# The choice of tokens in a four-layer kernel: lists in single instructions, a merge of minima and maxima, and an output norm in parts

## The chip, the cores and the metric

The kernel runs on one core of one Trainium2 chip as a single program. The metric is the device time in microseconds. The core has five engines with a queue each: TensorE (PE, with its weight loads shown as PEld), VectorE (DVE), ScalarE (ACT), GpSimd (POOL) and SyncE (SP), which issues most of the DMAs. Each engine works through its own queue in order; between engines there are semaphores.

## The reference

The input is 8 sequences of 512 rows of 256 numbers in float32. Four layers follow each other, and each adds a mixer and then a feed-forward part to the rows, both between layer norms. The change lies in the second layer. Its two parts are these, cut to what matters:

```python
# second mixer: 8 heads of 128, one common k and v, causal softmax
q = (x @ Wq + bq) + pe          # per head
k = kv[..., :128] + pe;  v = kv[..., 128:]
probs = softmax(causal(q @ k.T / sqrt(128)))
out = concat_heads(probs @ v) @ Wo
x = x + layernorm(out)

# second feed-forward part: 48 experts choose their tokens
xf = layernorm(x).reshape(4096, 256)
vals, idx = top_k((xf @ Wr.T).T, 128)       # 128 tokens for each of 48 experts
w = softmax(vals, axis=-1)
y = expert_mlp(xf[idx]) * w[..., None]      # gelu, 4 blocks of 256x256 and 256x64
out = zeros_like(xf).at[idx].add(y)
x = x + layernorm(out)
```

So every expert needs its 128 largest logits over all 4096 tokens, and no expert can start before the last sequence has left the mixer.

## The kernel before

The rows `X` stay in SBUF through the whole kernel, as 8 sequences of 128 partitions by 4 tiles by 256. The program is written in loops that are unrolled when it is built. A framework then orders each engine's queue: it lets an instruction go when what it needs is ready in its own account of the time, and prefers what comes earlier in the program. So the place of a step in the text is a rank and not a fixed slot.

**The mixer, `l1_attn`.** The outer loop runs over the sequences `b`, the next one over the heads `h`, the inner one over four query tiles `qt`. `scores` makes one matmul into PSUM (L927), a masked minimum on DVE (L932), the exponential with its sum on ACT (L936), a reciprocal on DVE (L937) and the scaling on POOL (L938). Two steps later `behind` transposes the tile on PE (L944) and copies it on ACT or DVE (L947, L949); after the fourth query tile `weigh` multiplies with V (L954, L957). After the eighth head `finish` projects with `wo` on PE (`project_out`, L193), and `add_norm` makes statistics (L105), an inverse root by three rounds of short DVE instructions (L90 to L96), `onb` (L170), four activations on ACT (L177) and one addition into `X` on POOL (L182). Between the heads, `front(b+1)` makes the next sequence's queries.

**The choice, class `Choice`.** Beside the attention of the following sequences, `logits` normalizes a finished sequence again, stores it to DRAM for the gathers, and makes its 48 router logits. The sequences go in five groups: (0,1), (2,3), (4,5), (6), (7). In a group, partitions 0 to 47 hold the experts' logits for the first sequence or half, and partitions 64 to 111 those of the second. `lists` takes the 128 largest of every row in 16 rounds of `max`, `max_index` and `match_replace` (L1076 to L1079). It is a generator: one step is one round of three instructions. `RATE[b]` is the number of steps that are placed in one head of sequence `b`, spread over its query tiles. A list ends with DMAs on SP that bring the upper half down (L1082, L1086) and copies into a table `TAB` of values and indices. From group 1 on, `merge` takes the 128 largest of the sorted lists so far in 16 more rounds of `max` and `match_replace` over 384 or 512 elements (L1110, L1112).

Group 4, the last sequence, has no attention to lie beside. In `l1_ffn`, after its logits and its list come its merge and then `slots`: exponentials and their sum; the softmax weights of all ten lists in `TAB` (POOL, L1132); the table's DMA to DRAM (L1133); the count of every list's entries above the 128th value; from the counts the place of each list's share; nine gathers of windows of the table (POOL, L1174), each followed by a predicated copy (L1180); two transposes, which give the weights `wT` and the token indices `iT`. Then the loop over the 48 experts starts with the gather of `xg` (L1229). Weights of three experts are loaded ahead on SP (L1225 to L1227).

In the mixer `add_norm` reads the projection from PSUM for the statistics and for the activations; it has two more arguments which another mixer uses:

```python
        t = pool.tile([P, NT, D], F32, tag=tag, name=f"yn{b}")
        for n, ps in enumerate(halves):                    # leave=True
            nc.scalar.copy(t[:, 2 * n:2 * n + 2, :], ps)
        if halves:
            ys = [t[:, n, :] for n in range(NT)]
        ...                                                # four activations
        m = NT // parts
        for n in range(0, NT, m):
            x = self.X[b][:, n:n + m, :]
            nc.gpsimd.tensor_tensor(x, x, t[:, n:n + m, :], ALU.add)
```

Of the kernel before, what the change touches and what calls it, by code (L numbers as in the profile page):

```python
# [9 lines left out]
F32 = mybir.dt.float32  # L10
# [858 lines left out]
def l1_attn(K):  # L869
# [10 lines left out]
    with ExitStack() as es:  # L880
# [14 lines left out]
        RATE = (0, 0, 1, 2, 3, 3, 5, 6)  # L895
# [63 lines left out]
        def finish(b):  # L959
            K.project_out(b, [(OT[b][:, h, :], wo[:, h, :]) for h in range(H)], pmm, "mm", s1)  # L960
# [41 lines left out]
class Choice:  # L1002
# [4 lines left out]

    E, NL, K = 48, 10, 128
    GROUPS = ((0, 1), (2, 3), (4, 5), (6,), (7,))

    def __init__(self, K):
# [10 lines left out]
        self.tab_d = dr.tile([E * NL * k, 2], F32, name="tab_d")  # L1022
# [15 lines left out]
        self.VV = cst.tile([E, NL, k], F32, name="VV")  # L1038
        self.TAB = cst.tile([E, NL * k, 2], F32, name="TAB")
        self.lg = {}  # L1040
        self.R = None
# [23 lines left out]
    def lists(self, g):  # L1065

        nc, E, k = self.kern.nc, self.E, self.K
        n = L if len(self.GROUPS[g]) == 2 else L // 2
        a = self.lg[g][:, 0:n]
        c = self.s1.tile([P, L], F32, tag="lg1", name=f"lga{g}")[:, 0:n]  # L1070
        val = self.sb.tile([P, k], F32, tag="val", name=f"val{g}")
        idx = self.sb.tile([P, k], U32, tag="idx", name=f"idx{g}")
        for r in range(k // 8):
            src, dst = (a, c) if r % 2 == 0 else (c, a)
            v8, i8 = val[:, 8 * r:8 * r + 8], idx[:, 8 * r:8 * r + 8]
            nc.vector.max(v8, src)  # L1076
            nc.vector.max_index(i8, v8, src)
            if r < k // 8 - 1:
                nc.vector.match_replace(dst, v8, src, -3.0e38)  # L1079
            yield  # L1080
        idf = self.sb.tile([P, k], F32, tag="idf", name=f"idf{g}")
        nc.sync.dma_start(out=self.VV[:, 2 * g + 1, :], in_=val[64:64 + E, :])  # L1082
        nc.vector.tensor_copy(idf, idx)
        nc.vector.tensor_scalar(idf, idf, self.first[:, g:g + 1], None, ALU.add)
        odd = self.sb.tile([E, k], F32, tag="odd", name=f"odd{g}")
        nc.sync.dma_start(out=odd, in_=idf[64:64 + E, :])  # L1086
        nc.vector.tensor_copy(self.VV[:, 2 * g, :], val[0:E, :])
        for j, t in enumerate((idf[0:E, :], odd)):
            lo = (2 * g + j) * k
            nc.gpsimd.tensor_copy(self.TAB[:, lo:lo + k, 1], t)  # L1090
        yield
        if g >= 1:
            yield from self.merge(g)

    def merge(self, g):

        nc, E, k = self.kern.nc, self.E, self.K
        if g == 1:
            lists = self.VV[:, 0:4, :]
        else:  # L1100
            nc.vector.tensor_copy(self.M[:, 1:3, :], self.VV[:, 2 * g:2 * g + 2, :])
            lists = self.M
        src = lists.rearrange("p l s -> p (l s)")
        n = src.shape[-1]
        two = [self.s1.tile([E, 4 * k], F32, tag=f"mg{j}", name=f"mg{g}_{j}")[:, 0:n]
               for j in range(2)]
        R = self.sb.tile([E, 3, k], F32, tag="R", name=f"R{g}")
        for r in range(k // 8):
            v8 = R[:, 0, 8 * r:8 * r + 8]
            nc.vector.max(v8, src)  # L1110
            if r < k // 8 - 1:
                nc.vector.match_replace(two[r % 2], v8, src, -3.0e38)  # L1112
                src = two[r % 2]
            yield
        self.M = R

    def slots(self, cst, sb, psum, ptag):

        K, nc = self.kern, self.kern.nc
        E, NL, k = self.E, self.NL, self.K  # L1120
        R = self.M[:, 0, :]

        nm = cst.tile([E, 1], F32, name="nm")
        nc.vector.tensor_scalar(nm, R[:, 0:1], -1.0, None, ALU.mult)
        sm = cst.tile([E, 1], F32, name="sm")
        ex = cst.tile([E, k], F32, name="ex")
        nc.scalar.activation(ex, R, AF.Exp, bias=nm, accum_out=sm)
        vv = self.VV.rearrange("p l s -> p (l s)")
        ev = cst.tile([E, NL * k], F32, name="ev")
        nc.scalar.activation(ev, vv, AF.Exp, bias=nm)  # L1130
        nc.vector.reciprocal(sm, sm)
        nc.gpsimd.tensor_scalar(self.TAB[:, :, 0], ev, sm, None, ALU.mult)  # L1132
        nc.sync.dma_start(  # L1133
            out=self.tab_d.rearrange("(e n) t -> e (n t)", e=E),
            in_=self.TAB.rearrange("p n t -> p (n t)"))

        thr = R[:, k - 1:k]
        cnt = []
        for op in (ALU.is_gt, ALU.is_ge):
            t = sb.tile([E, NL, k], F32, tag="cmp", name=f"cmp{len(cnt)}")  # L1140
            nc.vector.tensor_scalar(t.rearrange("p l s -> p (l s)"), vv, thr, None, op)
            c = cst.tile([E, NL], F32, name=f"cnt{len(cnt)}")
            nc.vector.tensor_reduce(c, t, AX.X, ALU.add)
            cnt.append(c)
        gt, eq = cnt
        nc.vector.tensor_tensor(eq, eq, gt, ALU.subtract)
# [13 lines left out]
        out = cst.tile([E, NL], F32, name="out")  # L1160
        nc.vector.tensor_tensor(out, end[:, 0:NL], end[:, 1:], ALU.subtract)
        nc.vector.tensor_scalar(out, out, float(k), None, ALU.add)

        at = cst.tile([E, NL], F32, name="at")
        nc.vector.tensor_tensor(at, self.start, end[:, 0:NL], ALU.subtract)
        ati = cst.tile([E, NL], U32, name="ati")
        nc.vector.tensor_scalar(at, at, 2.0, None, ALU.mult)
        nc.vector.tensor_copy(ati, at)
        got = cst.tile([E, k, 2], F32, name="got")
        nc.vector.tensor_copy(got, self.TAB[:, 0:k, :])  # L1170
        flat = self.tab_d.rearrange("n t -> (n t)")[:, None]
        for b in range(1, NL):
            t = cst.tile([E, 2 * k], F32, name=f"win{b}")
            nc.gpsimd.indirect_dma_start(  # L1174
                out=t, out_offset=None, in_=flat,
                in_offset=bass.IndirectOffsetOnAxis(ap=ati[:, b:b + 1], axis=0))
            m = cst.tile([E, k, 2], U8, name=f"from{b}")
            nc.vector.tensor_scalar(
                m, self.slot[:, :, None].to_broadcast([E, k, 2]), end[:, b:b + 1], None, ALU.is_ge)
            nc.vector.copy_predicated(got, m, t.rearrange("p (s t) -> p s t", t=2))  # L1180
        ps = psum.tile([P, 2, E], F32, tag=ptag, name="pgot")
        for j in range(2):
            nc.tensor.transpose(ps[:, j, :], got[:, :, j], K.ident[0:E, 0:E])
        wT = cst.tile([P, E], F32, name="wT")
        nc.vector.tensor_copy(wT, ps[:, 0, :])
        iT = cst.tile([P, E], U32, name="iT")
        nc.vector.tensor_copy(iT, ps[:, 1, :])
        return wT, iT

    def counters(self):  # L1190

        nc, cst, E, k = self.kern.nc, self.cst, self.E, self.K
        self.slot = cst.tile([E, k], F32, name="slot")
        self.start = cst.tile([E, self.NL], F32, name="start")
        for t, n, step, m in ((self.slot, k, 1, 0), (self.start, self.NL, k, self.NL * k)):
            i = self.s1.tile([E, k], I32, tag="io", name=f"io{m}")[:, 0:n]
            nc.gpsimd.iota(i, [[step, n]], base=0, channel_multiplier=m)
            nc.gpsimd.tensor_copy(t, i)

# [982 lines left out]
```

## Time and profile before

| What | Value |
|---|---|
| Median of 3 runs | 5109.19 us (5106.86 to 5115.65) |
| Profiled execution, its own time | 5105.01 us |
| Its span | 5103.3 us |
| Granted TensorE clock, mean | 0.933 |
| Busy: PE, DVE, ACT, POOL | 86%, 60%, 38%, 36% |
| First L932 of the mixer | 888.3 us from the span's start |
| Last L932 of the mixer ends | 1583.5 us |
| Last instruction of the last list ends | 1649.0 us |
| First gather of `xg` starts | 1694.6 us |
| Last gather of `xg` starts | 1983.3 us |

A line of the timeline has the start, the duration (of several alike, their stretch), the engine, the line of the kernel, the operation, what it writes and reads, the shapes and the count; in brackets the idle time before it and what ended it. A line of a table of windows has the stretch, its length, and each engine's busy time in it. Durations in groups are means of one instruction in nanoseconds. DVE's `max` appears as MAX8, `max_index` as a load and FIND_INDEX8, `match_replace` as a load and MATCH_REPLACE8; the masked minimum appears as CUSTOM_DVE_ANT_0.

### The profile page before, as it was taken

Reading aid. Unit: us, or ns where it says so; the run is one execution under the profiler, and the core shown is the slowest. Engines: PE = TensorE matmul, PEld = TensorE weight load, DVE = VectorE, ACT = ScalarE, POOL = GpSimd, SP = SyncE. Lnnn points to the kernel's source line nnn. Section 1 sums busy time; section 2 is a strip of 40 time slices with the busy share of each in tenths; the row PEclk is TensorE's granted clock in tenths of the full one; section 3 lists DMA queues with packets and bytes.
Section 4 is the critical chain, followed back from the end, with each engine's and each line's share of the span. In section 5 each row is a group of like instructions: output and inputs, shape, how many; then the busy total and the mean of one; then the engine's idle time right before and its main releaser. Section 6 shows DMA issues by size and latency. Waiting matters only on the chain.

```text
span 5103.3 us, 56570 instructions
## 1 busy us (share of the span) xinstructions
PE 4394.7 (86%) x18804; PEld 2694.8 (53%) x18804; DVE 3045.6 (60%) x8229; ACT 1958.5 (38%) x3835; POOL 1854.5 (36%) x1209
## 2 busy tenths in 40 slices
PE   8745788999895698899999999888888888799998
PEld 3334675555553697455555555433333333368884
DVE  6999746465778212666666543277777787751115
ACT  5411333434333233444444434365455555421112
POOL 0001212444433343211111110078778888803321
PEclk9877898999998899899999999999999999999999
DMA  4287421000001696000000000011111111126763
GB/s 114 79 198 177 130 64 56 5 5 9 5 14 40 171 249 173 5 5 5 5 5 5 1 21 1 1 54 45 42 44 44 50 46 42 56 71 226 235 206 103
DMA packets 401528, 357.89 MB, mean 70 GB/s; under 512 B 209394, under 2 KB 334020, under 8 KB 400676
## 3 DMA queue, kind: packets, MB, share of 16 engines
q1 hardware_dynamic: 373236, 305.83, 21.6%
q0 software_dynamic: 16320, 31.65, 2.2%
q10 hardware_dynamic: 11680, 16.80, 1.0%
q8 instruction: 149, 2.44, 0.2%
q14 instruction: 143, 1.17, 0.1%
HBM read 287.87 MB, written 66.09 MB: 69 GB/s over the span
## 4 chain that ended last, share of the span: by engine, by line
PE 37%; DVE 18%; issue 4%; POOL 4%; ACT 3%; DMA 1%; DVEq 0%; POOLq 0%; ACTq 0%; SPq 0%
DVE h L1730 7%; PE T L1432 5%; PE gb L1809 4%; DVE junk L1402 3%; PE h L1243 3%; PE g L1558 3%; PE y L1701 3%; PE yb L1823 2%; PE py L193 2%; DVE dB L1676 2%; PE pc L1623 2%; PE y L1254 2%; POOL h L1733 2%; PE o L1422 2%; PE pi L1609 1%
## 5 line engine op out<-in xcount | busy, mean ns | idle before, releaser
L1733 POOL TENSOR_TENSOR h<-h,C 128x1024 f32<-128x1024 f32 x256 | 595.8, 2354 | 175.6 <-DVE h L1730 141.9
L1701 PE MATMUL y<-h,C 128*128 128x512 f32 x1024 | 531.4, 660 | 107.1 <-POOL h L1733 107.1
L1730 DVE TENSOR_TENSOR_SCAN h<-dA,dB 128x512 f32<-128x512 f32 x512 | 589.0, 1203 | 29.4 <-ACT dA L1727 11.7
L1727 ACT ACTIVATE dA<-dl,A 128x512 f32<-128x512 f32 x512 | 352.5, 691 | 410.8 <-DVE h L1730 404.7
L1701 PEld LDWEIGHTS y<-h,C 128*128 128x128 f32 x1024 | 201.2, 208 | 414.5 <-issue 222.3
L938 POOL TENSOR_SCALAR p<-p,rs 128x128 f32<-128x128 f32 (+3 forms) x256 | 276.0, 1087 | 385.5 <-DVE rs L937 225.9
L1435 ACT ACTIVATE PT<-T 128x256 f32<-128x256 f32 (+3 forms) x512 | 212.1, 438 | 416.1 <-PE T L1432 396.0
L182 POOL TENSOR_TENSOR X<-X,yn 128x1024 f32<-128x1024 f32 (+1 forms) x80 | 154.1, 1932 | 590.3 <-ACT yn L177 529.3
L1397 PE MATMUL S<-KT,qz 128*128 128x512 f32 (+3 forms) x1024 | 326.0, 455 | 38.4 <-ACT qz L1385 16.9
L1432 PE MATMUL T<-qz,KT 128*128 128x512 f32 (+3 forms) x1024 | 318.1, 447 | 6.3 <-DVE mx L1402 4.2
L1437 POOL TENSOR_SCALAR_AFFINE_SELECT PT<-PT 128x512 f32<-128x512 f32 x128 | 81.8, 640 | 604.2 <-ACT PT L1435 599.8
L1681 POOL TENSOR_TENSOR dB<-du,B 128x2048 f32<-128x2048 f32 x64 | 289.6, 4525 | 0.1
L1402 DVE CUSTOM_DVE_ANT_0 junk<-S,mask 128x256 f32<-128x256 f32 (+3 forms) x512 | 249.8, 488 | 46.7 <-PE S L1397 2.6
L1397 PEld LDWEIGHTS S<-KT,qz 128*128 128x128 f32 x1024 | 178.5, 191 | 158.8 <-DVE mx L1402 36.7
L1809 PE MATMUL gb<-xbT,w_b 128*128 128x256 f32 (+1 forms) x1472 | 255.3, 332 | 1.0 <-ACT ts L2013 0.6
L1676 DVE TENSOR_TENSOR dB<-du,pb 128x2048 f32<-128x2048 f32 x64 | 145.4, 2273 | 167.2 <-PE pb L1673 117.5
L1815 DVE TENSOR_TENSOR hTb<-sb,gb 128x512 f32<-128x512 f32 x71 | 48.8, 687 | 325.4 <-PE gb L1809 325.4
L1809 PEld LDWEIGHTS gb<-xbT,w_b 128*128 128x128 f32 x1472 | 230.2, 191 | 23.1 <-ACT ts L2013 0.8
L1432 PEld LDWEIGHTS T<-qz,KT 128*128 128x128 f32 x1024 | 168.2, 191 | 121.5 <-issue 70.4
L936 ACT ACTIVATE p<-p,nm 128x128 f32<-128x128 f32 (+3 forms) x256 | 143.8, 563 | 198.5 <-DVE nm L932 193.3
L1248 ACT ACTIVATE hT<-h,w_l_ffn 128x128 f32<-128x128 f32 x384 | 109.8, 368 | 220.4 <-PE h L1243 220.4
L1243 PE MATMUL h<-xgT,w 128*128 128x128 f32 x1536 | 185.0, 279 | 0.0
(505 smaller groups left out, 9125.8 us busy)
## 6 DMA issues: line engine op xcount, KB each, us to landing
w_b<-l3f_w SPq DMA_DIRECT2D x138, 512.0 KB
w<-l1f_w SPq DMA_DIRECT2D x48, 1024.0 KB
C<-xdd SPq DMA_DIRECT2D x128, 256.0 KB
B<-xdd SPq DMA_DIRECT2D x64, 256.0 KB
w<-l1f_w SPq DMA_DIRECT2D x48, 256.0 KB
toep<-l0fd SPq DMA_DIRECT2D x32, 320.0 KB
X<-x SPq DMA_DIRECT2D x16, 512.0 KB
toep<-l0fd SPq DMA_DIRECT2D x32, 256.0 KB
```

The lines of the kernel that those rows point to most:

```text
L938: nc.gpsimd.tensor_scalar(p[:, 0:n], p[:, 0:n], rs, None, ALU.mult)
L1243: nc.tensor.matmul(ph[:, j, :], lhsT=w1[:, s, c, m * P:(m + 1) * P], rhs=xgT[:, c, :], start=(c == 0), stop=(c == 1))
L1397: nc.tensor.matmul(ps[:, 0:n], lhsT=QZ[:, j, qt * P:n], rhs=KT[:, g, 0:n], start=True, stop=True)
L1402: nc.vector.tensor_tensor_reduce(out=junk[:, 0:n], in0=tiles[j][:, 0:n], in1=mask[:, L - n:L], scale=1.0, scalar=-3.0e38, op0=ALU.add, op1 ...
L1432: nc.tensor.matmul(ps[:, 0:n], lhsT=KT[:, g, kt * P:(kt + 1) * P], rhs=QZ[:, j, kt * P:L], start=True, stop=True)
L1676: nc.vector.tensor_tensor(dB, du, pb[:, None, :].to_broadcast([P, 4, L]), ALU.mult)
L1681: nc.gpsimd.tensor_tensor(dB, du, B[:, None, :].to_broadcast([P, 4, L]), ALU.mult)
L1701: nc.tensor.matmul(py[2 * j + c], lhsT=K.ident, rhs=h[:, c, :], start=False, stop=(n == NS - 1))
L1727: nc.scalar.activation(dA, dl[:, c, :], AF.Exp, scale=A[:, c, n:n + 1])
L1730: nc.vector.tensor_tensor_scan(hs[-1][:, c % 2, :], dA, dB[:, c, :], 0.0, ALU.mult, ALU.add)
L1733: nc.gpsimd.tensor_tensor(h, h, C[:, None, :].to_broadcast([P, 2, L]), ALU.mult)
L1809: nc.tensor.matmul(ps[:, q, :], lhsT=ww[:, k, (c + q) * P:(c + q + 1) * P], rhs=xT[:, k, :], start=(k == 0), stop=(k == 1))
```

## The change

In the mixer, the projection's halves are copied from PSUM to SBUF on ACT before the activations read them, and the addition into `X` is made in four parts. `lists` yields after each instruction, and `RATE` counts instructions. The values are written into `VV` at once, the table `TAB` is kept on 128 partitions and holds raw values and indices, and each group's part goes to DRAM as soon as its list ends. Two sorted lists are merged by one maximum of the one with the reverse of the other, which leaves the 128 largest, and seven stages of a minimum and a maximum, which sort them again; the last list needs only the first of these. In `slots` the threshold is the minimum of the merged values, both halves are counted on 128 partitions, there are five gathers of 128 rows, the weights are computed from the gathered values, and each slot's share is picked by a product with a mask `own` and a matmul with `sel`, which adds the two halves and transposes. The diff, cut:

```diff
-        RATE = (0, 0, 1, 2, 3, 3, 5, 6)
+        RATE = (0, 0, 3, 5, 5, 5, 10, 9)
...
-            K.project_out(b, [(OT[b][:, h, :], wo[:, h, :]) for h in range(H)], pmm, "mm", s1)
+            K.project_out(
+                b, [(OT[b][:, h, :], wo[:, h, :]) for h in range(H)], pmm, "mm", s1, leave=True,
+                parts=4)
...
             nc.vector.max(v8, src)
+            yield
             nc.vector.max_index(i8, v8, src)
+            yield
             if r < k // 8 - 1:
                 nc.vector.match_replace(dst, v8, src, -3.0e38)
-            yield
+                yield
         idf = self.sb.tile([P, k], F32, tag="idf", name=f"idf{g}")
-        nc.sync.dma_start(out=self.VV[:, 2 * g + 1, :], in_=val[64:64 + E, :])
         nc.vector.tensor_copy(idf, idx)
-        nc.vector.tensor_scalar(idf, idf, self.first[:, g:g + 1], None, ALU.add)
+        nc.vector.tensor_scalar(
+            self.TAB[:, g, :, 1], idf, self.first[:, g:g + 1], None, ALU.add)
+        nc.scalar.copy(self.TAB[:, g, :, 0], val)
+        nc.sync.dma_start(
+            out=self.tab_d.rearrange("(p g s) t -> p g (s t)", p=P, g=len(self.GROUPS))[:, g],
+            in_=self.TAB[:, g].rearrange("p s t -> p (s t)"))
...
+        nc.vector.tensor_copy(odd, self.VV[64:64 + E, g, :])
         yield
-        if g >= 1:
-            yield from self.merge(g)
+        for j, x in enumerate((self.VV[0:E, g, :], odd)):
+            last = g == len(self.GROUPS) - 1 and j == 1
+            yield from self.merge(x, f"{g}_{j}", last)
...
+        if self.M is None:
+            self.M = x[:, ::-1]
+            return
+        t = self.sb.tile([E, k], F32, tag="mg", name=f"mg{uid}")
+        nc.vector.tensor_tensor(t, self.M, x, ALU.max)
+        s = k // 2
+        while s and not last:
+            u = self.sb.tile([E, k], F32, tag="mg", name=f"mg{uid}_{s}")
+            a, b = (v.rearrange("p (m h s) -> p m h s", h=2, s=s) for v in (t, u))
+            for h, op in enumerate((ALU.min, ALU.max)):
+                nc.vector.tensor_tensor(b[:, :, h, :], a[:, :, 0, :], a[:, :, 1, :], op)
+            t = u
+            s //= 2
+            if s in (16, 4, 1):
+                yield
+        self.M = t
+        yield
...
+        nc.vector.tensor_reduce(st[0:E, 0:1], R, AX.X, ALU.min)
+        nc.vector.tensor_copy(st[up, 0:1], st[0:E, 0:1])
...
+        for j, op in enumerate((ALU.is_gt, ALU.is_ge)):
+            t = cst.tile([P, G, k], F32, name=f"cmp{j}")
+            nc.vector.tensor_scalar(
+                t.rearrange("p l s -> p (l s)"), self.VV.rearrange("p l s -> p (l s)"),
+                st[:, 0:1], None, op)
+            nc.vector.tensor_reduce(cnt[:, j, :], t, AX.X, ALU.add)
...
-        for b in range(1, NL):
-            t = cst.tile([E, 2 * k], F32, name=f"win{b}")
+        for g in range(G):
+            t = cst.tile([P, k, 2], F32, name=f"win{g}")
             nc.gpsimd.indirect_dma_start(
...
+        pgot = [psum.tile([P, E], F32, tag=ptag, name=f"pgot{j}") for j in range(2)]
+        for j in (1, 0):
+            for g, t in enumerate(win):
+                v = sb.tile([P, k], F32, tag=f"v{j}", name=f"v{j}_{g}")
+                if j:
+                    nc.vector.tensor_tensor(v, t[:, :, 1], own[0][:, g, :], ALU.mult)
+                else:
+                    nc.scalar.activation(v, t[:, :, 0], AF.Exp, bias=st[:, 1:2])
+                    nc.vector.scalar_tensor_tensor(
+                        v, v, st[:, 2:3], own[0][:, g, :], ALU.mult, ALU.mult)
+                nc.tensor.matmul(
+                    pgot[j], lhsT=v, rhs=self.sel, start=(g == 0), stop=(g == G - 1))
```

## The prediction, made before the changed kernel ran

> **What bounds the kernel now.** The page's slices put the second mixer and its choice in slices 7 to 13 of 40. I cut that stretch with the table of windows. The edges are the moments at which DVE starts the masked minimum (L932) of head 0 of sequences 1 to 7. The columns are length, then busy time (and instructions) of PE, PEld, DVE, ACT and POOL, then the clock and DMA.
>
> ```profile
> core 0: us, PE busy (x) PEld busy (x) DVE busy (x) ACT busy (x) POOL busy (x), PEclk, DMA share, GB/s
> 957.60:1047.60 90.00, 84.49 (x354) 53.03 (x353) 42.41 (x194) 36.57 (x99) 38.28 (x34) 1.00 0.02 7
> 1047.60:1138.40 90.80, 85.07 (x355) 52.89 (x354) 64.93 (x255) 36.97 (x99) 38.14 (x34) 1.00 0.02 7
> 1138.40:1228.20 89.80, 84.47 (x354) 53.02 (x353) 49.65 (x213) 36.55 (x99) 38.88 (x36) 1.00 0.02 7
> 1228.20:1326.60 98.40, 87.28 (x354) 53.67 (x353) 71.91 (x277) 36.96 (x99) 38.84 (x36) 0.98 0.02 7
> 1326.60:1417.80 91.20, 84.46 (x354) 53.28 (x353) 61.42 (x236) 36.79 (x99) 38.34 (x34) 1.00 0.02 6
> 1417.80:1515.10 97.30, 87.14 (x354) 53.54 (x353) 72.69 (x282) 37.00 (x99) 38.83 (x36) 0.98 0.02 7
> ```
>
> PE sets the pace: a sequence without lists (1 and 3) takes 90 us. Sequences 4 and 6 take 8.4 and 7.3 us more, sequence 5 takes 1.2, sequence 2 only 0.8. In sequence 2 the list had 26.0 us of DVE (same table, tile `val` alone) at one round a head; in 4 it had 32.9 at three rounds a head. So list work in DVE's gaps is nearly free, and costs when it stands ahead of the attention's own instructions.
>
> After the last scores comes a tail. The windows from there to the first expert's gather:
>
> ```profile
> 1603.00:1612.40 9.40, 0.00 (x0) 0.00 (x0) 9.29 (x42) 0.04 (x1) 0.00 (x0) 0.61 0.00 0
> ...
> 1627.40:1650.60 23.20, 1.22 (x2) 0.50 (x2) 21.37 (x83) 0.00 (x0) 0.29 (x1) 0.53 0.33 90
> 1650.60:1669.60 19.00, 0.00 (x0) 0.00 (x0) 18.00 (x47) 1.36 (x1) 0.29 (x1) 0.50 0.01 1
> 1669.60:1680.10 10.50, 0.00 (x0) 0.00 (x0) 8.57 (x27) 1.78 (x3) 4.07 (x1) 0.50 0.23 47
> 1680.10:1694.60 14.50, 0.44 (x2) 0.31 (x2) 4.28 (x11) 0.00 (x0) 8.19 (x10) 0.50 0.14 31
> ```
>
> PE is idle: nothing else can run until the choice of tokens is known, so a microsecond off this chain is one off the span. In order: the last output norm; the last list; the last merge; counts and the table's way to memory; nine gathers. The timeline shows the first of these being held:
>
> ```profile
> 1610.28 0.55 DVE L1110 MAX8 R<-mg 48x8 f32<-48x384 f32 x1
> ...
> 1610.76 0.14 DVE L94 TENSOR_TENSOR onw<-onh,ony 128x4 f32<-128x4 f32 x1
> ...
> 1610.95 0.53 DVE L1112 MATCH_REPLACE8 mg<-R,mg 48x384 f32<-48x384 f32 x1
> ...
> 1612.17 0.16 DVE L170 SCALAR_TENSOR_TENSOR onb<-onmv,ony 128x4 f32<-128x4 f32 x1
> 1612.36 1.93 ACT L177 ACTIVATE yn<-py,onb,ony 128x256 f32<-128x256 f32 x4 [20.29 <-DVE onb L170]
> 1614.38 2.34 POOL L182 TENSOR_TENSOR X<-X,yn 128x1024 f32<-128x1024 f32 x1 [21.62 <-ACT yn L177]
> ```
>
> Group 3's merge alternates with the norm's short chain, and the one addition of 2.34 us waits for all four activations. Inside a sequence that addition has another effect (timeline of sequence 1):
>
> ```profile
> 986.71 2.36 POOL L182 TENSOR_TENSOR X<-X,yn 128x1024 f32<-128x1024 f32 x1
> ...
> 989.10 1.40 DVE L105 BATCH_NORM_STATS2 lnst<-X 128x6 f32<-128x256 f32 x4 [1.91 <-POOL X L182]
> ...
> 990.70 0.13 DVE L937 RECIPROCAL rs<-rs 128x1 f32<-128x1 f32 x1
> ...
> 991.00 2.78 POOL L938 TENSOR_SCALAR p<-p,rs 128x384 f32<-128x384 f32 x2 [1.94 <-DVE rs L937]
> ...
> 992.30 0.55 PE L944 MATMUL t<-C,p 128*128 128x128 f32 x3 [1.73 <-DVE lny L91]
> ```
>
> DVE waits for the addition, the reciprocals stand behind it, then POOL, then PE for 1.73 us.
>
> **Part 1, the choice after the last list.** Before: the last list instruction ends at 1649.0 and the first gather `xg` starts at 1694.58, 45.6 us. After, step by step:
> - Index cast, offset, copy of the upper half: 0.75 (from 1649.04 to 1649.58, and a 0.20 copy).
> - One full merge, 15 instructions. A TENSOR_TENSOR takes 0.16 us at 128x4 and 0.42 at 128x256 (L752), so 0.22 at 64 and 0.29 at 128 elements. Two independent ones start 0.08 apart at 128x4 (L90, L92), so about 0.15 here; a dependent one starts 0.035 after its predecessor's end. Seven stages of 0.15+0.22+0.035, and the maximum in front: 3.2. The last merge is one maximum, 0.33. Strided reads of one element are in no row; if they doubled it, 6.4.
> - Minimum (0.3) and its copy to the upper partitions (0.2).
> - Counts: 48x1280 took 4.45 us (1669.68 to 1674.13); 128x640 has half the length: 2.4.
> - Short chain to the indices: 2.1 before without its 0.75 of waiting, and four more copies of 0.15: 2.7.
> - Five gathers in place of nine. They have 128 rows like `xg`, whose issue takes 0.97 with 0.30 between: 4 x 1.27 = 5.1. The last lands 2.7 later (fastest `xg` landing; `win` of 48 rows: 2.4).
> - Product, matmul, cast: 1.0; to the gather's start 0.76, as now.
>
> Sum 19.5, with a hand-off to POOL 19.7: 25.9 us saved (20 to 29). The table's write leaves the path (5.2 us from 1674.9 to 1680.1): it is issued on SP in five pieces beside the merges; the last has the 8 us to the first gather, and SP's queue in front of it holds only weight loads that the windows show finished (DMA share 0.01 from 1640). Were that cover gone, up to 5.2 returns. Exponentials of the windows lie on ACT behind the gathers, and the weights are first used at the expert's scaling, 13 us after the first gather. The new sums, memsets and reciprocals lie in the gathers' shadow.
>
> A rule that speaks against splitting the merge: the Trainium skill, "VectorE: DVE Perf Modes", The DRAIN you can't avoid and Rules for kernel authors, says that the next instruction waits until the pipe is empty and that the count of instructions is to be kept low. With the fixed 150 cycles it gives, as an estimate, 223 ns for each of the fourteen halves without overlap, 3.4 to 3.7 us a merge and a sum half a microsecond longer; the rows above show independent short instructions overlapping, so they decide.
>
> **Part 2, the last output norm.** From the last statistics' end (1604.2) to `onb` (1612.33) are 8.1 us. The same chain undisturbed (1618.16 to 1620.9, and 0.2 for `onb`) takes 3.0. Group 3's list ends at 1589.9; its two merges, 0.75+6.4, end near 1597, before the last statistics at 1602.9. Saved 5.1; if the merges run late, 1. Four additions of 128x256: 1.26 (fastest) at 512 and 2.34 at 1024 elements give 0.72. They start after the first activation: 0.6+2.9+0.42 in place of 5.7 to the aggregation, 1.7 saved (0 if POOL's fixed cost is larger). The copies out of PSUM (0.59, L173) are done during the statistics. Together 6.8 (2 to 8.5).
>
> **Part 3, lists in the sequences.** A step is now one instruction, so the rates are 1, 1.7, 1.7, 1.7, 3.3 and 3 rounds a head for sequences 2 to 7, where it was 1, 2, 3, 3, 5 and 6. Sequence 2 stays. Sequence 4 falls to near sequence 2's rate, with 3.3 rounds waiting when its logits arrive instead of 6: its excess between 0.8 and 8.4; I take 3.4, so 5 saved. Sequence 5's excess was old merges (20.6 us of `R`): 1 saved. Sequence 6 keeps 3.3 rounds a head, as sequence 4 has now, and must also fit two merges that now spill into the long projection of sequence 7: 1 lost (3 saved to 5 lost). Sequence 7 is as before, since 27 instructions already wait when its list can start. All 56 steps of each group fit (58, 70, 60, 63 places). Sum 5 saved (12 to 5 lost).
>
> **Part 4, copy and four additions in sequences 0 to 6.** ACT gets two copies of 0.59 each, while idle for 14 us (961.8 to 976.4, waiting for the projection); queued behind them are only exponentials that need later PE work. Additions leave POOL as full as before (2.9 for 2.36). Three of four statistics come early, so the stall of 1.73 should lose about 0.8, seven times: 5.6 saved; bounds 12 saved, and 5 lost if the parts delay L938.
>
> **Sum.** 25.9 + 6.8 + 5 + 5.6 = 43.3. The profiled execution took 5105.0 us (span 5103.3 and 1.7 around it), so 5061.7. The runs' median, 5109.2, lies 4.2 above it; on that scale 5066. The experts' loop only starts earlier: PE is 98% busy in it (window 1695 to 2005).
>
> **Rivals.** *Slower: lists in front of the attention.* The finer steps stand between every two scores; if DVE then holds PE in each of sequences 2 to 7 as it does in 4 (8.4 each, 50), and seven merges of 3.4 come on top (24), against 19 of excess now, 55 is lost and 32.7 saved: 5132. It decides from 52 us of such stalls, 8.6 a sequence. Against it: the rates fall in five of six sequences. 5%.
> *The finer issue does nothing:* DVE's order follows readiness and not the place of a step (lists already run ahead of their places: group 0's 16 rounds take under five heads at one or two rounds a head). Then parts 3 and 4 give nothing: 32.7 saved, 5076. 20%.
> *The tail keeps a wait:* strided minima at twice the price and the table's landing on the path (3.2+5.2), and merges still inside the last norm (4): 31 saved with parts 3 and 4, or 17 if these lose 14 at their bounds: 5078 to 5092. 15%.
>
> **How the numbers follow.** The forecast has 56%, 4% are left for a time within 10 us of now through several of these. All bounds together reach 62 saved (29+8.5+12+12) and 12 saved (20+2-5-5); so 5047 and 5097, which take in the second and third rival and leave the slower one and half of the rest out. A difference of 0.2% (10 us) is about what a measurement can tell from none: faster 0.91, same 0.04, slower 0.05.
>
> **What would show it.** Right: about 20 us from the last FIND_INDEX8 to `xg`, five `win` gathers; from the last statistics to `onb` about 3 us; sequence 4 near 93 us; POOL additions of 0.7. Wrong: sequences 2 to 7 longer than now, merges of over 6 us, gathers released by the table's DMA.

## The result: 21.5 us faster, half of the forecast

The changed kernel takes 5083.38 us (median of 7 runs, 5077.73 to 5095.01), the kernel before 5104.93 (7 runs of the same session, 5102.91 to 5115.65): ratio 0.9954, 95% interval 0.9945 to 0.9963. Forecast were 5066 and a gain of 43.3. The profiled execution of the changed kernel took 5090.7 us (span 5089.0).

Both traces cut at the same events give this table. "Forecast" is the prediction's term for the stretch.

| Stretch (us) | before | after | difference | forecast |
|---|---|---|---|---|
| span's start to first L932 of the mixer | 888.3 | 893.8 | +5.5 | 0 |
| mixer, first L932 to end of last L932 | 695.1 | 703.6 | +8.5 | -10.6 (parts 3 and 4) |
| to the last output statistics | 20.7 | 19.2 | -1.5 | 0 |
| last output norm, to `onb` | 8.1 | 2.8 | -5.3 | -5.1 |
| last addition, to the last `lnst` | 5.8 | 4.0 | -1.8 | -1.7 |
| last list, to the last FIND_INDEX8 | 30.8 | 30.8 | 0 | 0 |
| choice, to the first gather `xg` | 45.6 | 21.7 | -23.9 | -25.9 |
| experts' loop | 308.2 | 308.1 | -0.1 | 0 |
| rest of the kernel | 3100.5 | 3104.9 | +4.4 | 0 |

The changed stretches sum to -24.0; the mixer is the one that went the wrong way. Its sequences 1 to 6 in the table of windows (columns as in the prediction):

```profile
core 0: us, PE busy (x) PEld busy (x) DVE busy (x) ACT busy (x) POOL busy (x), PEclk, DMA share, GB/s
963.00:1055.10 92.10, 85.69 (x354) 53.91 (x353) 42.33 (x193) 38.52 (x101) 38.80 (x37) 0.98 0.02 6
1055.10:1149.00 93.90, 86.11 (x354) 53.92 (x353) 67.11 (x259) 38.93 (x101) 38.82 (x37) 0.98 0.02 6
1149.00:1240.90 91.90, 85.82 (x355) 54.09 (x353) 50.44 (x224) 38.96 (x102) 38.83 (x37) 0.98 0.02 8
1240.90:1334.60 93.70, 86.03 (x354) 53.84 (x353) 66.41 (x259) 38.55 (x101) 38.77 (x37) 0.98 0.02 7
1334.60:1426.50 91.90, 84.46 (x355) 53.16 (x354) 53.26 (x239) 38.75 (x102) 38.83 (x37) 1.00 0.02 8
1426.50:1526.70 100.20, 86.86 (x355) 53.54 (x354) 74.32 (x295) 38.85 (x102) 39.09 (x37) 0.98 0.02 7
```

Sequences 1 and 3, which hold no list of their own, went from 90.0 and 89.8 to 92.1 and 91.9. Sequence 4 fell from 98.4 to 93.7, close to the forecast "near 93 us", but by luck: two misses cancel there, as e3 below shows with 88.9. So something lengthens even the sequences without a list of their own by 2 us, and under it the lists did better than forecast.

The tail is as forecast. Timeline from the merges to the last statistics:

```profile
1601.78 0.28 DVE L1111 TENSOR_TENSOR mg<-mg,VV 48x128 f32<-48x128 f32 x1
...
1602.18 2.67 DVE L1117 TENSOR_TENSOR mg<-mg 48x64 f32<-48x64 f32 x14
...
1619.47 2.07 ACT L177 ACTIVATE yn<-yn,onb,ony 128x256 f32<-128x256 f32 x4 [2.27 <-DVE onb L170]
1620.15 2.77 POOL L182 TENSOR_TENSOR X<-X,yn 128x256 f32<-128x256 f32 x4 [18.62 <-ACT yn L177]
1620.91 0.43 DVE L105 BATCH_NORM_STATS2 lnst<-X 128x6 f32<-128x256 f32 x1 [1.54 <-POOL X L182]
```

A merge takes 3.1 us (forecast 3.2) and is out of the way before the last statistics. Here, where POOL is idle, the four additions do what they are for: the first starts 0.68 after the first activation, and a statistic follows each. The choice behind the list:

```profile
1654.63 0.28 DVE L1111 TENSOR_TENSOR mg<-mg,VV 48x128 f32<-48x128 f32 x1
...
1663.16 0.17 DVE L1168 TENSOR_TENSOR at<-start,fe 128x5 f32<-128x5 f32 x1
1663.24 0.82 DVE L1189 TENSOR_TENSOR own<-slot,fe 128x640 f32<-128x640 f32 x1
1663.98 0.16 DVE L1170 TENSOR_SCALAR at<-at 128x5 f32<-128x5 f32 x1
1664.05 0.82 DVE L1189 TENSOR_TENSOR own<-slot,fe 128x640 f32<-128x640 f32 x1
1664.79 0.17 DVE L1171 CAST ati<-at 128x5 uint32<-128x5 f32 x1
...
1665.83 1.21 POOL L1176 DMA_INDIRECT win<-tab_d,ati  x1 [42.91 <-DVE own L1192]
...
1675.94 0.95 POOL L1253 DMA_INDIRECT xg<-xn_d,iT  x1 [3.88 <-issue]
```

Two comparisons for the masks `own`, 0.82 each, stand inside the three short instructions that make the indices, and the first gather starts 0.87 after the last index. The prediction had no term for the masks in front of the gathers, and 0.2 for the hand-off.

**Where the mixer waits.** Timeline at the end of sequence 1:

```profile
987.03 5.17 POOL L938 TENSOR_SCALAR p<-p,rs 128x256 f32<-128x256 f32 x5 [0.49 <-PE t L944]
...
989.02 2.08 ACT L177 ACTIVATE yn<-yn,onb,ony 128x256 f32<-128x256 f32 x4
...
992.17 2.77 POOL L182 TENSOR_TENSOR X<-X,yn 128x256 f32<-128x256 f32 x4
992.93 0.75 DVE L105 BATCH_NORM_STATS2 lnst<-X 128x6 f32<-128x256 f32 x2 [3.85 <-POOL X L182]
993.60 0.41 DVE L949 COPY PT<-t 128x256 f32<-128x256 f32 x1
...
994.15 0.74 PE L944 MATMUL t<-C,p 128*128 128x128 f32 x5 [2.36 <-DVE PT L949]
...
994.97 0.43 DVE L105 BATCH_NORM_STATS2 lnst<-X 128x6 f32<-128x256 f32 x1 [0.26 <-POOL X L182]
...
997.47 2.80 POOL L938 TENSOR_SCALAR p<-p,rs 128x384 f32<-128x384 f32 x2 [2.53 <-DVE rs L937]
```

The activations are done at 991.10, but POOL scales probabilities until 992.17. Only then do the additions begin, and all four run in one piece, 2.77 us where one took 2.36. DVE waits 3.85 us at the head of its queue for the first quarter (before: 1.91 for the whole), the copy L949 stands behind that, and PE stalls for 2.36 (before: 1.73).

### The profile page after: what moved, and what is told of

Same layout as the page of the kernel before. It is cut to its first block, busy times and chain, and to the rows that moved or that the text cites. A ratio compares the mean times of both kernels' runs of the same rounds, so it can differ in the third digit from the quotient of the medians.

```text
span 5089.0 us, 56574 instructions
## 1 busy us (share of the span) xinstructions
PE 4415.5 (87%) x18822; PEld 2714.2 (53%) x18822; DVE 3000.7 (59%) x8165; ACT 1974.5 (39%) x3860; POOL 1850.1 (36%) x1219
## 4 chain that ended last, share of the span: by engine, by line
PE 37%; DVE 18%; issue 5%; POOL 4%; ACT 3%; DMA 0%; DVEq 0%; POOLq 0%; SPq 0%; ACTq 0%
DVE h L1754 7%; PE T L1456 5%; PE gb L1833 4%; DVE junk L1426 4%; PE h L1267 3%; PE g L1582 3%; PE y L1725 3%; PE yb L1847 2%; PE py L193 2%; DVE dB L1700 2%; PE pc L1647 2%; PE y L1278 2%; POOL h L1757 2%; PE o L1446 1%; PE pi L1633 1%
## 5 line engine op out<-in xcount | busy, mean ns | idle before, releaser
L938 POOL TENSOR_SCALAR p<-p,rs 128x128 f32<-128x128 f32 (+3 forms) x256 | 276.7, 1089 | 416.3 <-DVE rs L937 259.8
L182 POOL TENSOR_TENSOR X<-X,yn 128x1024 f32<-128x1024 f32 (+2 forms) x104 | 157.4, 1528 | 589.4 <-ACT yn L177 526.7
L105 DVE BATCH_NORM_STATS2 onst<-py 128x6 f32<-128x256 f32 x160 | 60.9, 421 | 212.5 <-PE py L193 212.5
```

The source lines that it names most:

```text
L938: nc.gpsimd.tensor_scalar(p[:, 0:n], p[:, 0:n], rs, None, ALU.mult)
```

## The experiments

Theories after the result, with the letters that the expectations use. A: the later start of the mixer belongs to the execution; its rival B: the change moves it. C: the four additions in the sequences cost the 2 us. Its rivals: the copies out of PSUM do (D), or neither does, and the new steps or merges lengthen every sequence (E). All medians are of 4 to 9 runs, each ratio is against the kernel before on the same chip (5107 to 5112 us). "e3" and the like are the first parts of the labels.

| Run | us | ratio, 95% interval | mixer | sequences 1 to 6 |
|---|---|---|---|---|
| e0 | 5083.56 | 0.9952 [0.9938, 0.9965] | 703.3 | 92.0 93.9 91.8 93.7 91.8 100.1 |
| e1 | 5072.18 | 0.9927 [0.9914, 0.9941] | 683.8 | 90.8 89.3 89.8 89.7 89.8 96.9 |
| e2 | 5078.64 | 0.9941 [0.9927, 0.9954] | 700.0 | 92.1 92.1 91.8 91.9 91.8 100.5 |
| e3 | 5065.64 | 0.9916 [0.9902, 0.9930] | 683.7 | 90.0 89.3 89.8 88.9 89.8 98.4 |
| e4 | 5068.58 | 0.9917 [0.9903, 0.9930] | 684.1 | 90.1 89.3 89.9 89.0 89.9 98.4 |
| e6 | 5054.30 | 0.9895 [0.9880, 0.9910] | 673.9 | 90.0 89.3 89.8 88.9 89.8 88.9 |
| e7 | 5083.28 | 0.9938 [0.9924, 0.9952] | 693.8 | 90.8 90.8 89.8 98.1 89.8 97.0 |
| e8 | 5075.71 | 0.9930 [0.9917, 0.9944] | 690.5 | 90.8 90.8 89.8 92.7 89.8 98.9 |
| e9 | 5099.04 | 0.9975 [0.9965, 0.9985] | 714.8 | 94.8 92.7 94.8 93.8 94.4 103.0 |
| e11 | 5057.16 | 0.9892 [0.9876, 0.9908] | 677.7 | 90.4 90.2 90.2 89.6 90.2 89.6 |
| e12 | 5061.21 | 0.9904 [0.9888, 0.9920] | 680.7 | 90.8 90.6 90.6 90.0 90.6 90.0 |
| e13 | 5059.15 | 0.9902 [0.9885, 0.9919] | 673.8 | 90.0 89.3 89.8 88.9 89.8 88.9 |

### Four additions, copies, or neither

**e0**: the changed kernel once more.

> The changed kernel once more, as the measure for the others beside it. Its first profile had the mixer start 5.5 us later than before, in code that the change does not touch, with a granted clock of 0.75 in place of 0.91 between 740 and 780 us. Theory A (that shift is the execution's own): the start of the mixer lies within 1.5 us of 888 here, the time is about 5078 to 5084, 21 to 27 us under the kernel before. Theory B (the change moves it): the start is again near 894 and the time near 5090. In both, sequences 1 and 3 take 92 us and the stretch from the last FIND_INDEX8 to the first xg about 20 us.

The mixer starts at 885.2 instead of 893.8 (888 was expected), and its sequences have the same lengths to 0.1 us. The start belongs to the execution; the mixer's 8 us to the kernel.

**e1**: `leave=True, parts=1`. **e2**: `leave=False, parts=4`. **e3**: `leave=False, parts=1`, each in `finish`, for all sequences.

> The changed kernel with the addition into X in one part; the copies from PSUM stay. Theory C (the first quarter's statistics stand early in DVE's queue and wait for POOL, so the parts cost the 2 us): sequences 1 and 3 fall from 92 to 90 us, the last norm gets 1.7 us longer, the time falls by about 12 us to 5071. Theory D (the copies and the earlier release of PSUM change the order, so they cost the 2 us): sequences 1 and 3 stay at 92, the time rises by 2 to 5085.

> The changed kernel with the activations reading PSUM directly; the addition stays in four parts. Theory C (the parts cost): sequences 1 and 3 stay at 92 us, the time stays within 3 us of the changed kernel's. Theory D (the copies cost): sequences 1 and 3 fall to 90 and the time by 14 us to 5069.

> The changed kernel with the output norm of the mixer as before: no copy, one addition. Both theories C and D: sequences 1 and 3 return to 90 us, seven sequences give 14 us, the last norm costs 1.7 more, the time is 5071. A third theory E (the new steps of the lists or the new tiles change the order even where no list runs): sequences 1 and 3 stay at 92 and the time at 5083.

The four additions cost 16.3 us of mixer without the copies (e2 less e3) and 19.5 with them (changed kernel e0 less e1). Without the copies that is 2.0 to 3.0 in each of sequences 1 to 6. Beside one addition the copies leave the mixer's sum as it is (683.8 with, 683.7 without): sequences 1 and 4 are 0.8 longer in e1, each with a dip of the clock (last section), and sequence 6 is 1.5 shorter, which stays open. Beside four they add 3.3 (703.3 and 700.0), 1.8 of it in each of sequences 2 and 4; DVE's queue in the mixer then has another order, and why that costs is not shown. E is out: without the additions sequences 1 and 3 are at 90 again. Two times were missed: e2 is 4.9 under e0 where at most 3 was expected, and e3 is 5.4 under the expected 5071, as the additions cost more than the 14 us that both theories took. The table of waits, DVE in sequences 1 to 6, first the changed kernel and then e3 (sum, times, longest):

```profile
DVE lnst L105 <- POOL X L182: 24.6, 12, 3.9
```

```profile
DVE lnst L105 <- POOL X L182: 11.5, 6, 1.9
```

**e4**: `parts=4 if b == NB - 1 else 1`, no copies: four additions only where no attention follows.

> No copies; one addition in sequences 0 to 6 and four additions only behind the last sequence, where no attention follows. Theory C (the four additions cost inside the sequences, because the first quarter's statistics then stand earlier in DVE's queue): the sequences stay as in the kernel with one addition everywhere (mixer 684 +-1.5, sequence 1 at 90) and the tail gets its 1.8 us back (the stretch from `onb` to the last `lnst` 4.0 instead of 5.8): about 5064, 46 to 48 us under the kernel before of the same chip. Rival (part of the gain of one addition came from the tail or from another order of the whole queue): mixer over 688, time 5068 or more.

The mixer is e3's to 0.4 us and the last addition takes 3.9 instead of 5.8, as theory C wants. The medians don't show the 1.9 (ratios 0.9917 and 0.9916): it is less than they resolve, and e4's 5068.58 lies above the rival's mark of 5068, though its mixer does not.

### Why they cost

DVE's queue as it is built, behind the norm of sequence 1, shows the difference (L932 once for each minimum):

```
changed:  L937 x2, L105 x2 (X), L949, L105 x3, L107 x4, L932, ..., L932, ..., L937
e3:       L937 x2, L949, L932, L932, L105 x4 (X), L107 x4, L937, L949, ...
```

The framework takes the quarters of `X` to be ready early, as this order suggests (its own account of the time is not in the record), and ranks their statistics ahead of a copy and two masked minima. First test: make the four quarters ready together.

**e9**: no copies, four additions, and behind them in sequences 0 to 6:

```diff
+        if close:
+            x = self.X[b][:, :, 0:1]
+            nc.gpsimd.tensor_scalar(x, x, 1.0, None, ALU.mult)
```

> No copies, four additions everywhere; in sequences 0 to 6 a small POOL instruction (one column of each of the four tiles, times 1.0) follows the four additions, so that in the framework's account no statistics are ready before all four are done. POOL does a little more than in the changed kernel, but in the queue as built the statistics of sequence 1 stand behind L949 and one of the two masked minima, where the changed kernel has them in front of all three and the kernel with one addition behind all three. Theory C, cause in the place of the statistics: sequences 1 and 3 at 90 to 91, mixer 684 to 692, about 5066 to 5072. Rival (POOL's 2.9 us in four instructions instead of 2.4 in one is itself what costs): sequences 1 and 3 at 92 or more, mixer 700 to 705, about 5079 to 5084.

Both expectations missed: 94.8 us for sequences 1 and 3, and a median 15 us over the changed kernel's. The timeline of sequence 1 in that run (lines behind L182 are renumbered: L936 is the minimum, L941 the reciprocal, L942 the scaling, L948 the transpose, L953 the copy):

```profile
987.02 2.77 POOL L182 TENSOR_TENSOR X<-X,yn 128x256 f32<-128x256 f32 x4
989.89 0.23 POOL L185 TENSOR_SCALAR X<-X 128x4 f32<-128x4 f32 x1
...
992.04 1.25 POOL L942 TENSOR_SCALAR p<-p,rs 128x384 f32<-128x384 f32 x1 [1.93 <-DVE rs L941]
```

```profile
990.15 1.41 DVE L105 BATCH_NORM_STATS2 lnst<-X 128x6 f32<-128x256 f32 x4 [3.75 <-POOL X L185]
...
991.75 0.13 DVE L941 RECIPROCAL rs<-rs 128x1 f32<-128x1 f32 x1
...
992.05 0.68 DVE L936 CUSTOM_DVE_ANT_0 p<-S,mask 128x512 f32<-128x512 f32 x1
```

```profile
993.35 0.55 PE L948 MATMUL t<-C,p 128*128 128x128 f32 x3 [2.94 <-DVE lny L91]
```

The closing instruction moved the statistics behind L953 and one minimum only, and made the wait end later. What stands behind it is what matters, and I had looked at the wrong instructions: the reciprocal at 991.75, without which POOL scales nothing (idle 1.93) and PE transposes nothing (2.94 there). This run didn't separate place from POOL's time, so the next pair holds the queue fixed.

**e11** and **e12**: as e6 below, the statistics held until the minimum of head 2, query tile 3 is done, and the logits issued there instead of at the head's start. e11 has one addition, e12 has four.

```diff
+        def hold(b):
+            z = K.small.tile([P, 1], F32, tag="hold", name=f"hold{b}")
+            nc.vector.tensor_scalar(z, last[0], 0.0, None, ALU.mult)
+            x = K.X[b][:, :, 0]
+            nc.vector.tensor_scalar(x, x, z, None, ALU.add)
...
                     late.append((b, h, qt, scores(b, h, qt)))
+                    if b and (h, qt) == (2, 3):
+                        hold(b - 1)
+                        ch.logits(b - 1, s1, pmm, "mm")
```

> As the run with even rates (one addition, four in the last sequence), with the statistics of a finished sequence held back: two small DVE instructions (0 times a value that the masked minimum L932 of head 2, query tile 3 leaves, added to one column of X) make them wait for that minimum, and the router logits are issued after head 2's scores. In DVE's queue as built the first instruction that needs the addition then stands behind the first minimum of head 3, with the reciprocals of head 2 ahead of it. If the wait at the head of DVE's queue is what costs in this place: DVE's wait there (1.9 us before) falls under 0.7, PE's stall of 1.7 behind it too, sequences 1 to 5 at 88 to 89, mixer 662 to 670 instead of 674, 4 to 12 us under the run with even rates, about 5046. Rival (POOL, busy with the addition while scalings wait, stalls PE whatever stands in DVE's queue): within 3 us of the run with even rates, or slower by the later lists.

> As the run with the statistics held, and four additions in every sequence: around the end of a sequence DVE's queue as built is the same, instruction for instruction, as with one addition; only POOL's part differs (four of 0.73 instead of one of 2.36). If the place of the statistics in DVE's queue is what made the four additions cost 2 us a sequence: the mixer is within 4 us of the run held with one addition (POOL's 0.5 us more, seven times, is 3.7), the time within 5 us of it. Rival (POOL's longer time in itself, or its four hand-offs): sequences 1 and 3 longer by 1.5 or more, mixer longer by 10 to 16 us, time too.

With the same queue on DVE (in both traces the mixer's instructions there stand in the same order), four additions cost 0.4 us in each of sequences 1 to 6 and 3.0 in the mixer, where they cost 2.0 to 3.0 and 16.3 without the hold (e2 less e3, at the rates of the changed kernel). The 0.4 is POOL's longer time, 2.79 for 2.36. POOL in e12, then DVE, then POOL's one addition in e11 (lines renumbered: L948 is the held instruction):

```profile
982.18 2.79 POOL L182 TENSOR_TENSOR X<-X,yn 128x256 f32<-128x256 f32 x4
984.96 1.25 POOL L939 TENSOR_SCALAR p<-p,rs 128x384 f32<-128x384 f32 x1
```

```profile
985.01 0.55 DVE L948 TENSOR_SCALAR X<-X,hold 128x4 f32<-128x4 f32 x1 [1.83 <-POOL X L182]
```

```profile
985.68 2.36 POOL L182 TENSOR_TENSOR X<-X,yn 128x1024 f32<-128x1024 f32 x1
988.03 1.24 POOL L939 TENSOR_SCALAR p<-p,rs 128x384 f32<-128x384 f32 x1
```

Here POOL goes on to a scaling at once, because its reciprocal was ahead of the held instruction. So of the 2 to 3 us a sequence, 0.4 is POOL's time, and the rest goes with the place of the statistics in DVE's queue.

As an improvement the hold failed: the mixer takes 677.7 where 662 to 670 was expected, and in e11 the held instruction still waits 1.40 us for the addition, where under 0.7 was expected. PE's stall of 1.74 before it is gone, but smaller ones (0.25, 0.63, 0.19, 0.40, 0.83, 0.40) follow; e11's sequences 1 to 6 sum to 3.3 more than e6's, its projection stretch is 2.0 shorter, and the ratios are equal.

### Lists: rate, step and merge

**e7**: the choice and the merges alone, on e3: one round a step again, `RATE = (0, 0, 1, 2, 3, 3, 5, 6)`.

> The new choice and the merges by minima and maxima, with one addition and no copies in the mixer, and the lists as before: steps of a round at 0, 0, 1, 2, 3, 3, 5, 6 rounds a head. Tells what of the mixer's 11 us came from the merges alone and what from the new steps and rates. Theory: the merges give the 1 to 2 us of sequence 5 (its old merge had 20.6 us of DVE) and the tail gives 23.9 + 5.3; sequence 4 keeps about 98 and the mixer is 690 to 696, the time about 5078 (30 to 34 us under the kernel before of the same chip). Rival (sequence 4 was long because of the old merge and its DMAs, not because of the list's rate): sequence 4 at 92 or less, mixer under 687, time under 5072.

29.2 us under its chip's 5112.45 (ratio 0.9938), with sequence 4 at 98.1 still and sequence 5 1.4 shorter. So the tail with the merges is worth about 30 for a forecast of 31.0 (25.9 and 5.1; the 1.7 of the last additions are not in e7), and steps and rates are worth 10.1 of mixer (e7 less e3), of which 0.8 is a dip of the clock in e7's sequence 1 (last section).

**e8**: on e3, one round a step, `RATE = (0, 0, 1, 2, 2, 2, 3, 3)`.

> As the run with one addition and no copies, but a step is again a round of three instructions, at the rates 0, 0, 1, 2, 2, 2, 3, 3 rounds a head (with single instructions it was 1, 1.7, 1.7, 1.7, 3.3, 3 rounds). Separates the grain of a step from the rate. If the rate alone made sequence 4 shorter: sequence 4 at 89 to 91, mixer 683 to 686, time within 2 us of the run with one addition and no copies (about 5066). If single instructions matter in themselves: sequence 4 at 94 or more, mixer 688 or more, time 5070 or more.

Sequence 4 at 92.7: of its 9.2 us, 5.4 come from going from three rounds a head to two, 3.8 from single instructions at 1.7 rounds. So neither expectation for sequence 4 held (89 to 91, or 94 and more); the mixer of 690.5 and the time are on the side of the single instructions (688 and 5070 or more). Grain and rate aren't fully separated, as the rates were not quite equal; in sequence 6 the grain made no difference (98.9 at 3 rounds, 98.4 at 3.3).

**e6**: on e4, the rates made even.

```diff
-        RATE = (0, 0, 3, 5, 5, 5, 10, 9)
+        RATE = (0, 0, 3, 5, 5, 5, 5, 12)
```

> As the run with parts only behind the last sequence, and the rates 0, 0, 3, 5, 5, 5, 5, 12 instead of 0, 0, 3, 5, 5, 5, 10, 9: sequence 6 runs at sequence 5's rate and 26 of its instructions spill into sequence 7. If the rate (instructions a head) sets a sequence's excess: sequence 6 falls from 98.4 to 90 to 91, sequence 7 (68.2) grows by 0 to 2, time 5 to 8 us under the sibling, about 5058. Rival (sequence 6 is long because of the merges and the second norm that fall there, whatever the rate): it stays over 95 and the time within 2 us of the sibling's; or the spill only moves the cost, and sequence 7 takes what sequence 6 gives.

Sequence 6 falls by 9.5 us to 88.9, and sequence 7 takes 28.1 us of list work in place of 19.0 and gets no longer (67.9). The mixer gains 10.2, and the median is 14.3 under e4's, where 5 to 8 was expected; the profiled executions lie 14.2 apart, and 3.9 of that stands ahead of the mixer, where the edit changes nothing. At 56.6 us under the one before of its chip it has the lowest median here; e11 and e13, which have the same rates, are within its noise. The reason is seen in head 5 of the list's sequence: first e7's sequence 4, then e3's sequences 4 and 6, then e6's sequence 6.

```profile
1299.70:1311.90 12.20, 9.59 (x34) 5.04 (x34) 11.49 (x37) 4.17 (x11) 4.28 (x5) 1.00 0.00 0
```

```profile
1287.90:1295.40 7.50, 7.50 (x31) 4.33 (x30) 7.36 (x25) 3.72 (x11) 3.91 (x4) 1.00 0.00 0
...
1468.20:1480.50 12.30, 9.59 (x34) 5.03 (x34) 11.59 (x38) 4.17 (x11) 4.38 (x5) 1.00 0.01 2
```

```profile
1459.90:1467.40 7.50, 7.50 (x31) 4.35 (x30) 7.36 (x25) 3.70 (x11) 3.92 (x4) 1.00 0.01 2
```

With a round between every two scores (8.4 us of list a head) DVE is busy for 11.5 of 12.2 us and sets the pace; with 3.7 PE is busy all the time. DVE becomes the bound of single heads long before its share of a sequence says so.

### The masks in the choice

**e13**: e6, with the masks computed from a copy of the ranks that needs the scaled starts.

```diff
+        f2 = cst.tile([P, G, 2], F32, name="f2")
+        nc.vector.scalar_tensor_tensor(
+            f2, at[:, :, None].to_broadcast([P, G, 2]), 0.0, fe, ALU.mult, ALU.add)
...
-                fe[:, :, j:j + 1].to_broadcast([P, G, k]), op)
+                f2[:, :, j:j + 1].to_broadcast([P, G, k]), op)
```

> As the run with even rates; in the choice the masks `own` are computed from a copy of the ranks that needs the scaled starts (f2 = 0 times at, plus fe), so that in DVE's queue as built the index chain L1168, L1170, L1171 stands in one piece and both comparisons with the ranks (L1189, 0.82 each in the changed kernel) behind it. If they were what made the choice 21.7 us instead of the predicted 19.7: the stretch from the last FIND_INDEX8 to the first `xg` falls by 1.3 to 2.0, to 19.7 to 20.4, the masks still ready before the first gather lands; the time 1 to 2 us under the run with even rates, less than can be measured, so the stretch decides. Rival (the gather waits for the masks' product in any case, or the later masks now hold the products behind the gathers): the stretch stays within 0.5 of 21.7.

```profile
1631.17 0.17 DVE L1170 TENSOR_SCALAR at<-at 128x5 f32<-128x5 f32 x1
1631.37 0.17 DVE L1171 CAST ati<-at 128x5 uint32<-128x5 f32 x1
...
1632.42 1.86 POOL L1176 DMA_INDIRECT win<-tab_d,ati  x1 [42.45 <-DVE f L1188]
```

A miss, at the border that the rival named. From the last FIND_INDEX8 to the first gather it is 10.4 us instead of 11.6, but that gather then takes 1.86 instead of 1.21, and the stretch is 21.2 for 21.7. Why the first gather grows stays open.

## Why the prediction was right and wrong

**Part 1, right.** 23.9 for 25.9. Of the 2.0 missing, 1.2 are the masks that stand in front of the indices (e13), a term that the sum did not have, and 0.7 the hand-off to POOL, which took 0.87 for 0.2. Merge, counts, gathers and landing are each within 0.2. Of the rules on the merge, the rows decided rightly: a half is shown with 0.21 us (median of L1117 in the changed kernel), and fourteen of them take 2.67, 0.19 each, so independent ones overlap. The Trainium skill ("VectorE: DVE Perf Modes", The DRAIN you can't avoid) has the next instruction wait for an empty pipe, from which the estimate of 0.223 each came, but adds that one that is not held starts earlier; this trace agrees with the addition.

**Part 2, right.** 5.3 and 1.8 for 5.1 and 1.7. The projection ahead of it gave another 1.5, which was not in the sum (0.6 in e3, whose mixer ends without part 4's stalls).

**Part 3, the right mechanism, the wrong size.** Without part 4's stalls it is worth 11.4 of mixer (before less e3) for 5, near the bound of 12. Its terms: sequence 5 -1.4 (forecast -1) and sequence 6 +1.1 (+1) were right; sequence 4 is the one mis-sized, -9.5 for -5. I kept an excess of 3.4 there because a backlog of instructions waits when its logits arrive; at 1.7 rounds a head no excess is left (88.9, less than a sequence without lists). Sequence 2, put at nothing, gave 1.5.

**Part 4, the step that failed.** Forecast -5.6, bounds 12 saved and 5 lost; the runs show 16.3 lost by the additions alone and 19.5 beside the copies. "Three of four statistics come early" was taken from the addition's length alone. The same timeline of before shows POOL scaling until the addition starts at 986.71, over a microsecond after the last activation has ended:

```profile
983.70 3.04 POOL L938 TENSOR_SCALAR p<-p,rs 128x512 f32<-128x512 f32 x3
...
984.87 0.57 ACT L177 ACTIVATE yn<-py,onb,ony 128x256 f32<-128x256 f32 x1
```

There is no idle POOL into which parts could move forward. So the parts end 0.4 later than the whole on the chip, but by the order of the queue earlier in the framework's account, which puts DVE's statistics in front of work that PE needs. The lower bound was named for a delay of L938, which is the right sort of loss (POOL's L938 waits 2.53 behind a reciprocal), but its size was near POOL's 0.54 taken seven times, and not that of the queue held up behind it.

Put together: -23.9 - 5.3 - 1.8 - 1.5 for the tail, -11.4 and +19.5 to +19.9 in the mixer give -24; the rest of the kernel and the start differ by execution. That the time lies inside the range of 5047 to 5097 is in part luck: part 4 lies 11 to 15 beyond its lower bound, and part 3's 6.4 above its term took some of that back.

**The rivals.** "The finer issue does nothing" and "the tail keeps a wait" gave times near the measured one (5076, 5078 to 5092) for reasons that did not happen: the finer issue did much, the tail kept no wait. The slower rival's stalls came in every sequence from 1 to 6, but at 1.7 to 4.8 us (changed kernel e0 less e3) and not 8.4, and from the additions. Its mark was also stated wrongly: 52 us is the sum of its stalls and its 24 of merges, so stalls of about 28, some 4.6 a sequence, would have decided it.

## What to carry to other kernels

Before an operation is cut into parts so that its reader can start early, look at when its engine is free: if it begins late for lack of its engine, as here, parts only make it longer. With queues whose order comes from a model, a result that the model believes to be early can move its readers to the head of an in-order queue; compare the queue as built on both sides, and ask what is behind the first instruction that waits. Filler work is to be spread by the engine's time in each single head, not over the whole: 10 us lay in two entries of a table of rates.

## What the runs showed of the hardware

A stall can be followed by a dip of the granted clock. In the changed kernel, after PE's 2.36 us, ten microseconds of sequence 1 read:

```profile
993.00:1003.00 10.00, 8.51 (x35) 5.44 (x35) 8.62 (x50) 4.64 (x12) 5.32 (x6) 0.83 0.01 2
```

That is 1.7 us of clock lost. The Trainium skill ("TensorE: Matmul & The Clock Gate", Part 1: The HAM clock gate) tells of half the clock after an idle window of about 3.4 us, in windows that run freely; half the clock over a window of that length would be, as an estimate, the 1.7. The runs agree in the free phase (sequence 5 of the changed kernel has the same stall of 2.36 and shows 1.00), but not in a whole idle window: PE stalls of 2.36 us, and of 1.73 in sequence 1 of e7, were enough.

What a dip costs differs. Sequences 3 and 5 of the changed kernel both last 91.9 us (in the first table) with 0.98 and 1.00 granted, PE 85.82 and 84.46 busy. So there the price of the four additions is the wait, not the clock. Behind the shorter stall of one addition a dip does cost. Sequence 1 holds no list, and its instructions stand in the same order on all four engines in e7 and e3; here it is in e7, then in e3:

```profile
967.00:1057.80 90.80, 85.45 (x354) 54.11 (x353) 42.41 (x193) 36.58 (x99) 38.23 (x34) 0.98 0.02 7
```

```profile
959.00:1049.10 90.10, 84.58 (x355) 53.10 (x354) 42.47 (x194) 36.65 (x99) 38.27 (x34) 1.00 0.02 7
```

It is 90.0 to 90.1 in the kernel before, e3, e4, e6 and e13, without a dip, and 90.8 in e1, e7 and e8, with one. So 0.8 us of a sequence can differ between two executions of the same code.

Code that no edit touched varies by more than some of the edits: the first L932 comes between 883.1 and 897.8 us over these profiles, and the kernel behind the experts' loop takes 3100.5 to 3108.2. Between 700 and 880 us the clock is 0.91 in e6 (first L932 at 883.1) and 0.88 in e7 (897.8), so part of it may go with the clock; the cause stays open. The profiled executions of e1 and e3 have an equal mixer and lie 12.1 us apart (their medians 6.5): 4.6 of it comes ahead of the mixer and 7.2 behind the loop. That is why single stretches decide here rather than medians.
